# Slot blocks, residual adds and projections in a two-layer graph kernel

## Chip, core and metric

The kernel runs on one core of a Trainium2 chip. The metric is the device time of one execution in microseconds, the median of repeated runs; a profile is one more execution, recorded by the hardware profiler.

The core's engines run side by side and meet through semaphores: PE (TensorE, matrix products into PSUM), DVE (VectorE), ACT (ScalarE), POOL (GpSimd) and SP (which issues the DMAs). Each takes its instructions strictly in the order in which the program lists them, so an instruction that waits holds up all behind it on its engine.

## What is computed

128 graphs of 128 nodes with 64 features each. `adj` is a weighted adjacency; about one entry in sixteen is not zero. Layer 0 sums, over the neighbours k of node j, a hidden vector of 192 ReLUs, and projects the sum; layer 1 is a matrix product with `adj` and a small network. Both are residual with a layer norm.

```python
mask = (adj > 0.0)
xj_proj = x @ W1a
diff = x[:, :, None, :] - x[:, None, :, :]
h = relu(xj_proj[:, :, None, :] + diff @ W1b + b1)      # 128 x 128 x 192 a graph
hm = einsum('bjkh,bjk->bjh', h, mask)
x = layernorm(x + hm @ W2 + deg[..., None] * b2)
...
agg = einsum('bmn,bnd->bmd', adj, x)
h = elu(agg @ V1 + c1); h = elu(h @ V2 + c2)
out = layernorm(x + h @ V3 + c3)
```

The argument of the ReLU is A[j] + C[k], with A = x (W1a + W1b) + b1 and C = -x W1b. So layer 0 needs, for each node and each of its neighbours, relu(A[j] + C[k]).

## The kernel before, in words

**Pairs and slots.** Two graphs make a pair; there are 64 pairs, and the work is laid out by pair. `prepare` finds each node's degree, ranks the nodes by it and builds a permutation (`permb`, `permT`); `sort_x` and `sort_mask` sort features and mask, so that node position 0 has the most neighbours. A node at sorted position p gets a fixed number of slots, one for each neighbour it may have, from the table

```python
BANKS = (((72, 128, 9),), ((30, 72, 12),), ((0, 8, 22), (8, 30, 15)))
```

An entry (p0, p1, s) is a block: positions p0 to p1 with s slots each, s x (p1 - p0) columns. The blocks of one inner tuple share a PSUM bank[...]. In all E = 1514 columns.

**One-hot columns.** `sort_mask` computes with a prefix matmul the running number of each neighbour (`vp`), and compares it on DVE with each slot's number (`slotc`): `oh` (L572) has a one where neighbour k of position p falls into slot s. One compare per block, for both graphs at once.

**Units.** The hidden dimension is cut in three columns c: 0 and 1 are the first 128 channels of either graph, 2 holds the last 64 of both. A unit is (pair, c, bank): nine a pair. ACT seeds the bank `e` with A[j], repeated over the slots (L714, one instruction per block); PE adds C[k] by gathering with the one-hot columns, three bf16 parts of C in turn (L725 for c = 0 and 1, three matmuls; L729 for c = 2, six half-width ones); DVE reduces |A + C| over the slots (L739, one instruction per block). Since relu(z) = (z + |z|)/2 the linear part is added later, and an empty slot leaves |A|. What empty slots contribute is taken off by `corr`: `short` (L520 to L528) builds with matmuls 2 x (slots - degree), PSUM gets it by a constant matmul of `small` with `srow2` (L523) and by matmuls of -2 with the sorted mask (L525, L527); DVE multiplies by max(A, 0) (L532), POOL subtracts A x slots (L518, L538). Four banks (`edges`, NE = 4) go round, so four units are under way.

**Projection of A.** `project_a` (L498) computes A for the three columns by three matmuls of all 128 rows with zero-padded weights `wap` and `wah` (L504) into one bank, and ACT adds b1 in two instructions (L509, L511).

**Finish.** `finish` (L636): POOL forms hm (L642) from the sums and corr once the pair's nine units are reduced, PE projects with W2, ACT copies, and `unsort` (L661) puts the rows back in the order of the input, adding x by a matmul with the identity (L662). `norm` (L594) copies the result out on ACT (L597), takes the statistics on DVE from PSUM (L603, L605), POOL raises to -1/2 (L610), DVE and ACT apply (L613, L619). Then come the product with `adj` (`aggregate`), two ELU layers (`hidden1`, `hidden2`) and `last` (L692), which adds x1 again by an identity matmul (L694), and the second `norm`.

**The order.** No scheduler of the compiler decides it. `Flow` is a planner in the kernel: each step names its engine, an assumed cost in us, what it comes after and how many of the four general PSUM banks (`m0` to `m3`) it takes. It emits the step that can start first by its own clock, among near ones the one due first. ROUND (13.0) sets the pace at which pairs are due, AHEAD = 3 how many pairs earlier preparation begins. "POOL PORT" and "DVE PORT" steps are kept apart on the planner's clock. The emitted order is fixed; on the chip each engine follows it. `load` issues a pair's two DMAs, `finish` the two stores.

**The dense part.** Where a node had more neighbours than slots, `dense` would compute its pair again without slots; it starts with a test over all pairs (L792 to L800).

Of the kernel before, what the change touches and what calls it, by code (L numbers as in the profile page):

```python
# [39 lines left out]
EPS = 1e-5  # L40


BANKS = (((72, 128, 9),), ((30, 72, 12),), ((0, 8, 22), (8, 30, 15)))


@with_exitstack
def gnn_kernel(ctx: ExitStack, tc: tile.TileContext, x, adj, w1, b1, w2, b2,
# [74 lines left out]
    nc.vector.memset(onesf, 1.0)  # L122
    onesb = const([P, 2 * P], BF16, "onesb")
    nc.vector.memset(onesb, 1.0)
    small = const([P, P], BF16, "small")
    nc.vector.memset(small, 1.0 / P)
# [5 lines left out]
    mtwoh = const([P, 2, P], BF16, "mtwoh")  # L132
    nc.vector.memset(mtwoh, 0.0)
    for s in range(2):
        nc.vector.memset(mtwoh[:, s, s * HB:(s + 1) * HB], -2.0)
    mone = const([P, 1], F32, "mone")
    nc.vector.memset(mone, -1.0)

# [45 lines left out]
    srow2 = const([P, 3, P], BF16, "srow2")  # L184
    nc.vector.tensor_scalar(srow2, srow, 2.0, None, op0=OP.mult)

    wa = temp([P, H], F32, "wa")
# [162 lines left out]
def sparse(tc, env):  # L350
# [18 lines left out]
    EV = {}  # L369


    ROUND = 13.0
    AHEAD = 3
    PACE = ROUND / (3 * NB)
    STEP = 1.3
# [34 lines left out]
    def flat(t):  # L410
        return t.rearrange("p s n -> p (s n)")

    def prepare(p):

        a = ADJ[p]
        d = S[p] = {}
        mk = d["mk"] = prep.tile([P, 2, N], BF16, name="mk")
        ev, = yield ("POOL PORT", pool(2 * N) + 0.2, [event("load", p)], 0,
                     lambda: nc.gpsimd.tensor_scalar(mk, a, 0.0, None, op0=OP.is_gt))  # L419
        deg = prep.tile([P, 2], F32, name="deg")  # L420
        ev, = yield ("DVE", dve(2 * N), [ev], 0,
                     lambda: nc.vector.tensor_reduce(deg, mk, AX.X, OP.add))
# [24 lines left out]

        def permute():
            for s in range(2):
                nc.vector.tensor_scalar(permb[:, s, :], g.iotb, pos[:, s:s + 1], None,  # L450
                                        op0=OP.is_equal)
        ev, = yield ("DVE PORT", 0.36, [ev], 0, permute)
        flow.start(due(p, 7), STEP, sort_x(p, ev))
        flow.start(due(p, 7), STEP, sort_mask(p, ev))

# [42 lines left out]
    def project_a(p, xT, ev):  # L498

        d = S[p]  # L500

        def project(aps):
            for c, w in enumerate((g.wap[:, 0, :], g.wap[:, 1, :], g.wah)):
                nc.tensor.matmul(aps[:, c * N:(c + 1) * N], w, xT[:, 1, :], start=True, stop=True)  # L504
        ev, aps = yield ("PE", 0.66, [ev], 1, project)
        aj = d["aj"] = prep.tile([P, 3, N], F32, name="aj", bufs=6)

        def bias():
            nc.scalar.activation(flat(aj[:, 0:2, :]), aps[:, :2 * N], AF.Identity,  # L509
                                 bias=g.b1c[:, 0:1])  # L510
            nc.scalar.activation(aj[:, 2, :], aps[:, 2 * N:3 * N], AF.Identity,  # L511
                                 bias=g.b1c[:, 1:2])
        ev, = yield ("ACT", act(2 * N, 1) + act(N, 1), [ev], 0, bias)
        flow.give(aps, ev)
        happened(ev, "aj", p)
        have = ev
        sa = prep.tile([P, 3, N], F32, name="sa")
        evs, = yield ("POOL PORT", 1.0, [have], 0, lambda: nc.gpsimd.tensor_mul(sa, aj, g.srow))  # L518

        def short(eb):  # L520

            mtp = d["mtp"]
            nc.tensor.matmul(eb[:, :3 * N], g.small, g.srow2.rearrange("p c n -> p (c n)"),  # L523
                             start=True, stop=False)
            nc.tensor.matmul(eb[:, :2 * N], g.mtwo, flat(mtp), start=False, stop=False)  # L525
            for s in range(2):
                nc.tensor.matmul(eb[:, 2 * N:3 * N], g.mtwoh[:, s, :], mtp[:, s, :],  # L527
                                 start=False, stop=(s == 1))  # L528
        ev, eb = yield ("PE", 0.38, [have, event("mtp", p)], 1, short)
        ea = prep.tile([P, 3, N], F32, name="ea")  # L530
        ev, = yield ("DVE", dve(3 * N), [ev], 0,
                     lambda: nc.vector.scalar_tensor_tensor(  # L532
                         ea, aj, 0.0, eb[:, :3 * N].rearrange("p (c n) -> p c n", c=3),
                         op0=OP.max, op1=OP.mult))
        flow.give(eb, ev)

        corr = d["corr"] = prep.tile([P, 3, N], F32, name="corr", bufs=7)
        ev, = yield ("POOL PORT", 1.05, [ev, evs], 0, lambda: nc.gpsimd.tensor_sub(corr, ea, sa))  # L538
        happened(ev, "corr", p)

    def sort_mask(p, ev):
# [49 lines left out]
        flow.give(t, ev)  # L591
        happened(ev, "adjT", p)

    def norm(yps, ev, name):  # L594

        y = work.tile([P, 2, O], F32, name="y", bufs=6)
        evy, = yield ("ACT", act(2 * O), [ev], 0, lambda: nc.scalar.copy(flat(y), yps[:, :2 * O]))  # L597
        st = work.tile([P, 2, 3], F32, name="st", bufs=12)
        ve = work.tile([P, 2], F32, name="ve", bufs=12)

        def stats():

            nc.vector.bn_stats(st.rearrange("p s t -> p (s t)"),  # L603
                               yps[:, :2 * F].rearrange("p (s f) -> p f s", s=2))
            nc.vector.tensor_scalar(ve, st[:, :, 2], 1.0 / F, EPS, op0=OP.mult, op1=OP.add)  # L605
        ev, = yield ("DVE", 0.38, [ev, evy], 0, stats)
        flow.give(yps, ev)
        rs = work.tile([P, 2], F32, name="rs", bufs=12)
        ev, = yield ("POOL PORT", 0.72, [ev], 0,
                     lambda: nc.gpsimd.tensor_tensor(rs, ve, g.mhalf, op=OP.pow))  # L610
# [25 lines left out]
    def finish(p):  # L636
# [22 lines left out]
        nc.sync.dma_start(g.degs[:, 2 * p:2 * p + 2], ys[:, 2 * O:])  # L659

        def unsort(t):  # L661
            nc.tensor.matmul(t[:, :2 * O], ident, flat(xx), start=True, stop=False)  # L662
            for s in range(2):
                nc.tensor.matmul(t[:, s * O:(s + 1) * O], d["permT"][:, s, :],  # L664
                                 ys[:, s * O:(s + 1) * O], start=False, stop=(s == 1))
# [25 lines left out]

        def last(t):  # L692
            nc.tensor.matmul(t[:, :2 * O], onesb[:, :P], flat(g.c3p), start=True, stop=False)
            nc.tensor.matmul(t[:, :2 * O], ident, flat(x1), start=False, stop=False)  # L694
            for s in range(2):
                nc.tensor.matmul(t[:, s * O:(s + 1) * O], h2[:, s * N:(s + 1) * N], g.v3s,
                                 start=False, stop=(s == 1))
        ev, t = yield ("PE", 0.83, [ev], 1, last)
# [278 lines left out]
```

## Time and profile before

| | |
|---|---|
| median of 3 runs | 928.74 us (928.43 to 929.03) |
| the profiled execution | 928.32 us |
| its span, first to last instruction | 925.7 us |
| first gather starts, last one ends | 42.2 us, 902.4 us |
| PE busy | 867.1 us (94%), 6739 instructions |
| DVE busy | 813.8 us (88%), 2278 instructions |
| ACT busy | 717.3 us (77%), 2050 instructions |
| POOL busy | 506.6 us (55%), 654 instructions |
| DMA | 18.84 MB, 20 GB/s, q1 8.1% of 16 engines |

The span is a fill (loads, set-up, preparation of the first pairs), 64 rounds of one pair each with all stages of different pairs beside each other, and a drain. Busy is the union of an engine's instructions; PE's ends are modelled, so its starts are the safer reading. In groups by line, the columns behind the bar are busy us, mean ns of one, and idle time of the engine before them with what ended it. DVE's and ACT's instructions overlap the next by some 80 ns where nothing holds it.

### The profile page before, as it was taken

The page shows a single profiled execution, that of the slowest core. Times are in us where ns is not written, and L with a number is a line of the kernel's source. Part 1 is how long each engine was busy: PE and PEld are TensorE (multiplying, and loading weights), DVE is VectorE, ACT ScalarE, POOL GpSimd, SP SyncE. Part 2 cuts the span into 40 slices and gives each one's busy share as a digit, 9 for nine tenths or more (in the row PEclk, how much of TensorE's full clock was granted, in tenths as well). Part 3 has the DMA queues.
Part 4 walks back from the last instruction along what each step waited for, and adds up shares of the span by engine and source line. Part 5 has one row for each costly group of instructions (what it writes and reads, how often), then busy time and mean ns, then how long its engine had stood idle before and what let it go on. Part 6 is the DMA issues. An engine that isn't in the chain of part 4 may idle for free. (4 is left out here: it accounts for less than half of the span.)

```text
span 925.7 us, 19643 instructions
## 1 busy us (share of the span) xinstructions
PE 867.1 (94%) x6739; PEld 556.4 (60%) x6740; DVE 813.8 (88%) x2278; ACT 717.3 (77%) x2050; POOL 506.6 (55%) x654
## 2 busy tenths in 40 slices
PE   2689999999999999999999999999999999999994
PEld 1456666665665665666665666666666666666663
DVE  7699889989989989989989989999999999999972
ACT  0577887788788788788788788888878887888772
POOL 1565555665556565556565556565556555555521
PEclk9999999999999999999999999999999999999996
DMA  1100100100110110110100010110011001000000
GB/s 29 43 10 21 25 15 21 24 21 16 24 24 13 24 24 14 24 25 12 25 23 15 22 24 12 25 24 16 21 25 24 16 21 25 16 23 22 7 8 12
DMA packets 63580, 18.84 MB, mean 20 GB/s; under 512 B 46257, under 2 KB 63474, under 8 KB 63474
## 3 DMA queue, kind: packets, MB, share of 16 engines
q1 hardware_dynamic: 63474, 17.52, 8.1%
q8 instruction: 55, 0.90, 0.4%
q14 instruction: 51, 0.42, 0.1%
HBM read 13.24 MB, written 4.19 MB: 19 GB/s over the span
## 5 line engine op out<-in xcount | busy, mean ns | idle before, releaser
L739 DVE TENSOR_REDUCE sums<-e 128x56 f32<-128x504 f32 (+3 forms) x768 | 395.0, 542 | 33.6 <-PE e L725 16.9
L714 ACT COPY e<-aj 128x504 f32<-128x504 f32 (+2 forms) x768 | 366.1, 486 | 74.3 <-DVE sums L739 67.4
L725 PE MATMUL e<-oh,cp 128*128 128x504 bf16 (+1 forms) x1152 | 281.7, 375 | 1.8 <-ACT e L714 1.7
L610 POOL TENSOR_TENSOR rs<-ve,mhalf 128x2 f32<-128x2 f32 x128 | 90.6, 708 | 228.2 <-DVE ve L605 223.9
L725 PEld LDWEIGHTS <-cp 128*128 128x128 bf16 x1152 | 106.1, 97 | 89.5 <-DVE sums L739 1.1
L729 PE MATMUL e<-oh,cp 128*64 128x504 bf16 (+1 forms) x1152 | 157.5, 382 | 1.1 <-ACT e L714 1.1
L572 DVE TENSOR_TENSOR oh<-vp,slotc 128x1008 bf16<-128x1008 bf16 (+2 forms) x256 | 153.9, 601 | 3.2 <-ACT vp L564 3.0
L642 POOL TENSOR_TENSOR hm<-sums,corr 128x384 f32<-128x384 f32 x64 | 73.6, 1151 | 45.8 <-DVE sums L739 42.3
L629 ACT ACTIVATE e<-m,mone 128x256 f32<-128x256 f32 x128 | 62.6, 489 | 32.4 <-PE m L688 30.9
L493 POOL CAST cp<-r 128x512 bf16<-128x512 f32 x64 | 48.9, 765 | 70.5 <-DVE r L490 70.4
L729 PEld LDWEIGHTS <-cp 128*64 128x64 bf16 x1152 | 53.9, 109 | 42.9 <-issue 18.2
L495 POOL TENSOR_TENSOR cp<-r,cp 128x512 bf16<-128x512 f32 x64 | 74.5, 1164 | 5.0
L518 POOL TENSOR_TENSOR sa<-aj,srow 128x384 f32<-128x384 f32 x64 | 64.4, 1007 | 21.2 <-ACT aj L511 21.1
L538 POOL TENSOR_TENSOR corr<-ea,sa 128x384 f32<-128x384 f32 x64 | 67.2, 1050 | 3.6 <-DVE ea L532 2.6
L419 POOL TENSOR_SCALAR mk<-adj 128x256 bf16<-128x256 f32 x64 | 54.8, 856 | 21.3 <-DMA xx<-in_x_dram 20.9
L632 DVE SCALAR_TENSOR_TENSOR h<-e,m 128x256 f32<-128x256 f32 x128 | 52.5, 410 | 10.1 <-ACT e L629 9.3
L490 DVE TENSOR_TENSOR r<-m,cp 128x256 f32<-128x256 f32 x128 | 53.1, 416 | 6.5 <-ACT cp L486 6.1
L597 ACT COPY y<-m 128x128 f32<-128x128 f32 x128 | 33.4, 261 | 28.7 <-PE m L664 22.0
L619 ACT ACTIVATE o<-y,nb,rs 128x64 f32<-128x64 f32 x128 | 51.2, 467 | 3.0 <-DVE nb L613 3.0
L486 ACT CAST cp<-m 128x256 bf16<-128x256 f32 x128 | 49.5, 388 | 3.2 <-PE m L479 3.2
L619 ACT ACTIVATE x<-y,nb,rs 128x64 f32<-128x64 f32 x128 | 49.3, 433 | 3.3 <-DVE nb L613 1.6
L651 PE MATMUL m<-w2h,hm 128*128 128x64 f32 x256 | 48.1, 289 | 0.0
(189 smaller groups left out, 1731.5 us busy)
## 6 DMA issues: line engine op xcount, KB each, us to landing
adj<-in_adj_dram SPq DMA_DIRECT2D x64, 128.0 KB, 2.3
xx<-in_x_dram SPq DMA_DIRECT2D x64, 64.0 KB, 2.2
out_dram<-o SPq DMA_DIRECT2D x64, 64.0 KB, 1.7
degs<-ys SPq DMA_DIRECT2D x64, 1.0 KB, 1.7
w1a<-in_L_gnn_W_dram SPq DMA_DIRECT2D x2, 48.0 KB, 2.2
w1b<-in_L_gnn_W_dram SPq DMA_DIRECT2D x2, 48.0 KB, 2.1
v1d<-in_L_gnn_W_dram SPq DMA_DIRECT2D x2, 32.0 KB, 2.1
v2s<-in_L_gnn_W_dram SPq DMA_DIRECT2D x1, 64.0 KB, 2.0
```

The lines of the kernel that those rows point to most:

```text
L495: lambda: nc.gpsimd.tensor_sub(cp[:, 2], r1, cp[:, 1]))
L518: evs, = yield ("POOL PORT", 1.0, [have], 0, lambda: nc.gpsimd.tensor_mul(sa, aj, g.srow))
L538: ev, = yield ("POOL PORT", 1.05, [ev, evs], 0, lambda: nc.gpsimd.tensor_sub(corr, ea, sa))
L572: lambda: nc.vector.tensor_tensor(oh[:, :, c].rearrange("p b (s w) -> p b s w", w=w), vp[:, :, p0:p1].rearrange("p b (o w) -> p b o w", o= ...
L610: lambda: nc.gpsimd.tensor_tensor(rs, ve, g.mhalf, op=OP.pow))
L619: nc.scalar.activation(o[:, s, :], y[:, s, :], AF.Identity, bias=nb[:, s:s + 1], scale=rs[:, s:s + 1])
L629: lambda: nc.scalar.activation(e, z, AF.Exp, bias=g.mone))
L642: lambda: nc.gpsimd.tensor_sub(hm, d["sums"], d["corr"]))
L714: nc.scalar.copy(e[:, off:off + sl * w].rearrange("p (s w) -> p s w", w=w), d["aj"][:, c:c + 1, p0:p1].to_broadcast([P, sl, w]))
L725: nc.tensor.matmul(e[:, :n], cp[:, k, c, 0:P], oh[:, c, base:base + n], start=False, stop=(k == 2), skip_group_check=True)
L729: nc.tensor.matmul(e[s * HB:(s + 1) * HB, :n], cp[:, k, s, P:H], oh[:, s, base:base + n], start=False, stop=(k == 2), skip_group_check=True)
L739: nc.vector.tensor_reduce(d["sums"][:, c, p0:p1], e[:, off:off + sl * w].rearrange("p (s w) -> p w s", w=w), AX.X, OP.add, apply_absolute_ ...
```

## The change

- **Six blocks.** Still three banks, now each with two blocks; E = 1355 columns. Seeds, compares and reductions are one instruction per block, so eighteen, six and eighteen a pair.
- **Residuals on POOL.** `unsort` and `last` lose the identity matmul. `norm` gets `rest`: ACT copies PSUM into y and gives the bank back, POOL adds `rest`, DVE takes the statistics from y.
- **A by row tiles.** For c = 0 and 1 two matmuls of 64 rows each, on the two halves of the array's rows, into two banks; `wah` as before; ACT adds b1 in three instructions.
- **Empty-slot factor.** POOL computes `free` = sorted mask - slots/128 in bf16; `short` is one matmul of -2 with it and two half-width ones. `small`, `srow2`, `mtwoh` go.
- ROUND becomes 11.8, and assumed costs in the planner change with the steps.

```diff
-BANKS = (((72, 128, 9),), ((30, 72, 12),), ((0, 8, 22), (8, 30, 15)))
+BANKS = (((34, 65, 11), (0, 3, 22)), ((65, 99, 9), (3, 15, 16)), ((15, 34, 13), (99, 128, 7)))
...
+    sfrac = const([P, 2, P], BF16, "sfrac")
+    nc.vector.tensor_scalar(sfrac, srow[:, 0:2, :], 1.0 / P, None, op0=OP.mult)
...
-    ROUND = 13.0
+    ROUND = 11.8
...
-        def project(aps):
-            for c, w in enumerate((g.wap[:, 0, :], g.wap[:, 1, :], g.wah)):
-                nc.tensor.matmul(aps[:, c * N:(c + 1) * N], w, xT[:, 1, :], start=True, stop=True)
-        ev, aps = yield ("PE", 0.66, [ev], 1, project)
+        def project(*aps):
+            for s in range(2):
+                k = slice(s * F, (s + 1) * F)
+                nc.tensor.matmul(aps[s][:, 0:N], g.wa[k, 0:P], xT[k, 1, :], start=True, stop=True)
+            nc.tensor.matmul(aps[0][:, N:2 * N], g.wah, xT[:, 1, :], start=True, stop=True)
+        ev, *aps = yield ("PE", 0.5, [ev], 2, project)
...
-            mtp = d["mtp"]
-            nc.tensor.matmul(eb[:, :3 * N], g.small, g.srow2.rearrange("p c n -> p (c n)"),
-                             start=True, stop=False)
-            nc.tensor.matmul(eb[:, :2 * N], g.mtwo, flat(mtp), start=False, stop=False)
-            for s in range(2):
-                nc.tensor.matmul(eb[:, 2 * N:3 * N], g.mtwoh[:, s, :], mtp[:, s, :],
-                                 start=False, stop=(s == 1))
-        ev, eb = yield ("PE", 0.38, [have, event("mtp", p)], 1, short)
+            free = d["free"]
+            nc.tensor.matmul(eb[:, :2 * N], g.mtwo, flat(free), start=True, stop=True)
+            for s in range(2):
+                nc.tensor.matmul(eb[s * HB:(s + 1) * HB, 2 * N:3 * N], g.mtwo[:, :HB],
+                                 free[:, s, :], start=True, stop=True)
+        ev, eb = yield ("PE", 0.2, [have, event("free", p)], 1, short)
...
+        free = d["free"] = prep.tile([P, 2, N], BF16, name="free")
+        evf, = yield ("POOL PORT", 0.7, [evm], 0,
+                      lambda: nc.gpsimd.tensor_sub(free, mtp, g.sfrac))
+        happened(evf, "free", p)
...
-        evy, = yield ("ACT", act(2 * O), [ev], 0, lambda: nc.scalar.copy(flat(y), yps[:, :2 * O]))
+        ev, = yield ("ACT", act(2 * O), [ev], 0, lambda: nc.scalar.copy(flat(y), yps[:, :2 * O]))
+        flow.give(yps, ev)
+        ev, = yield ("POOL PORT", 0.45, [ev], 0, lambda: nc.gpsimd.tensor_add(y, y, rest))
...
             nc.vector.bn_stats(st.rearrange("p s t -> p (s t)"),
-                               yps[:, :2 * F].rearrange("p (s f) -> p f s", s=2))
+                               y.rearrange("p s f -> p f s"))
...
         def unsort(t):
-            nc.tensor.matmul(t[:, :2 * O], ident, flat(xx), start=True, stop=False)
             for s in range(2):
                 nc.tensor.matmul(t[:, s * O:(s + 1) * O], d["permT"][:, s, :],
-                                 ys[:, s * O:(s + 1) * O], start=False, stop=(s == 1))
-        ev, t = yield ("PE", 0.6, [ev, event("permT", p)], 1, unsort)
-        x1, ev = yield from norm(t, ev, "x1")
+                                 ys[:, s * O:(s + 1) * O], start=True, stop=True)
+        ev, t = yield ("PE", 0.42, [ev, event("permT", p)], 1, unsort)
+        x1, ev = yield from norm(t, ev, "x1", xx)
...
             nc.tensor.matmul(t[:, :2 * O], onesb[:, :P], flat(g.c3p), start=True, stop=False)
-            nc.tensor.matmul(t[:, :2 * O], ident, flat(x1), start=False, stop=False)
...
-        o, ev = yield from norm(t, ev, "o")
+        o, ev = yield from norm(t, ev, "o", x1)
```

More of the change, by code (lines that the diff above doesn't have):

```diff
@@ L124, in gnn_kernel @@
     nc.vector.memset(onesb, 1.0)
-    small = const([P, P], BF16, "small")
-    nc.vector.memset(small, 1.0 / P)
     mhalf = const([P, 2], F32, "mhalf")
@@ L131, in gnn_kernel @@
     nc.vector.memset(mtwo, -2.0)
-    mtwoh = const([P, 2, P], BF16, "mtwoh")
-    nc.vector.memset(mtwoh, 0.0)
-    for s in range(2):
-        nc.vector.memset(mtwoh[:, s, s * HB:(s + 1) * HB], -2.0)
     mone = const([P, 1], F32, "mone")
@@ L183, in gnn_kernel @@
         nc.vector.memset(srow[:, :, p0:p1], float(s))
-    srow2 = const([P, 3, P], BF16, "srow2")
-    nc.vector.tensor_scalar(srow2, srow, 2.0, None, op0=OP.mult)
-    wa = temp([P, H], F32, "wa")
+    sfrac = const([P, 2, P], BF16, "sfrac")
+    nc.vector.tensor_scalar(sfrac, srow[:, 0:2, :], 1.0 / P, None, op0=OP.mult)
+    wa = const([P, H], F32, "wa")
     nc.vector.tensor_add(wa, w1a, w1b)
@@ L451, in permute @@
                                         op0=OP.is_equal)
-        ev, = yield ("DVE PORT", 0.36, [ev], 0, permute)
+        ev, = yield ("DVE PORT", 0.45, [ev], 0, permute)
         flow.start(due(p, 7), STEP, sort_x(p, ev))
@@ L500, in project_a @@
         d = S[p]
-        def project(aps):
-            for c, w in enumerate((g.wap[:, 0, :], g.wap[:, 1, :], g.wah)):
-                nc.tensor.matmul(aps[:, c * N:(c + 1) * N], w, xT[:, 1, :], start=True, stop=True)
-        ev, aps = yield ("PE", 0.66, [ev], 1, project)
+        def project(*aps):
[4 more added lines that the diff above has]
+        ev, *aps = yield ("PE", 0.5, [ev], 2, project)
         aj = d["aj"] = prep.tile([P, 3, N], F32, name="aj", bufs=6)
         def bias():
[L509 to L514, printed above, removed]
+            for c in range(3):
+                nc.scalar.activation(aj[:, c, :], aps[c % 2][:, (c // 2) * N:(c // 2 + 1) * N],
+                                     AF.Identity, bias=g.b1c[:, c // 2:c // 2 + 1])
+        ev, = yield ("ACT", 3 * act(N, 1), [ev], 0, bias)
+        for t in aps:
+            flow.give(t, ev)
         happened(ev, "aj", p)
@@ L592, in turn, with norm @@
         happened(ev, "adjT", p)
-    def norm(yps, ev, name):
+    def norm(yps, ev, name, rest):
         y = work.tile([P, 2, O], F32, name="y", bufs=6)
-        evy, = yield ("ACT", act(2 * O), [ev], 0, lambda: nc.scalar.copy(flat(y), yps[:, :2 * O]))
+        ev, = yield ("ACT", act(2 * O), [ev], 0, lambda: nc.scalar.copy(flat(y), yps[:, :2 * O]))
+        flow.give(yps, ev)
+        ev, = yield ("POOL PORT", 0.45, [ev], 0, lambda: nc.gpsimd.tensor_add(y, y, rest))
         st = work.tile([P, 2, 3], F32, name="st", bufs=12)
@@ L603, in stats @@
             nc.vector.bn_stats(st.rearrange("p s t -> p (s t)"),
-                               yps[:, :2 * F].rearrange("p (s f) -> p f s", s=2))
+                               y.rearrange("p s f -> p f s"))
             nc.vector.tensor_scalar(ve, st[:, :, 2], 1.0 / F, EPS, op0=OP.mult, op1=OP.add)
-        ev, = yield ("DVE", 0.38, [ev, evy], 0, stats)
-        flow.give(yps, ev)
+        ev, = yield ("DVE", 0.4, [ev], 0, stats)
         rs = work.tile([P, 2], F32, name="rs", bufs=12)
@@ L697, in last @@
                                  start=False, stop=(s == 1))
-        ev, t = yield ("PE", 0.83, [ev], 1, last)
-        o, ev = yield from norm(t, ev, "o")
+        ev, t = yield ("PE", 0.54, [ev], 1, last)
+        o, ev = yield from norm(t, ev, "o", x1)
         nc.sync.dma_start(g.out[2 * p:2 * p + 2].rearrange("b j f -> j b f"), o)
```

## The prediction

> **What bounds the kernel now.** I read the busy times first, then the windows of the steady part (600 to 800 us), the waits of PE and DVE in it, the timeline of PE over some microseconds and last the groups by shape.
>
> ```profile
> 600.00:800.00 200.00, 197.74 (x1574) 128.23 (x1569) 182.77 (x510) 165.07 (x480) 116.00 (x150) 1.00 0.09 21
> ```
>
> The columns are PE, weight loads, DVE, ACT, POOL, then granted clock and DMA. PE is busy 98.9%, DVE 91.4%, ACT 82.5%, POOL 58%. Since the ends of matmuls are modelled, 98.9% alone proves nothing; the starts do.
>
> ```profile
> 314.11 0.80 PE L725 MATMUL e<-oh,cp 128*128 128x504 bf16 x3
> 314.75 0.41 PE L646 MATMUL m<-w2d,hm 128*128 128x128 f32 x2
> 315.00 0.25 PE L650 MATMUL m<-cp,mtp 128*128 128x64 bf16 x3
> ```
>
> Three gathers of 504 columns start 0.64 us before the next work does: 213 ns each, and the next instruction starts at once. PE works without a break. In the same 200 us it waited 1.2 us in all, while DVE's longest waits are
>
> ```profile
> DVE deg L422 <- POOL mk L419: 7.2, 15, 0.5
> DVE sums L739 <- PE e L729: 4.2, 16, 0.3
> DVE sums L739 <- PE e L725: 2.5, 15, 0.2
> ```
>
> So PE bounds, DVE follows 7% behind. One pair of graphs is one round; its end shows on POOL:
>
> ```profile
> 603.79 1.37 POOL L642 TENSOR_TENSOR hm<-sums,corr 128x384 f32<-128x384 f32 x1 [0.68 <-DVE sums L739]
> ...
> 617.17 1.37 POOL L642 TENSOR_TENSOR hm<-sums,corr 128x384 f32<-128x384 f32 x1 [0.68 <-DVE sums L739]
> ```
>
> 13.38 us per round here. L642 runs from 55.3 to 903.4 us, 63 rounds of 13.46 on the average (about 13.86 between 313 and 550 us). So the span is 55.3 + 63 x 13.46 + 22.3 = 925.7, and the profiled run 928.32, 2.6 more; the median shown, 928.74, is 0.4 above it. A change counts as one from 0.2% (1.9 us). Work per round, DVE and POOL less their 20 and 8 us of set-up: PE 867/64 = 13.5, DVE 794/64 = 12.4, ACT 717/64 = 11.2, POOL 499/64 = 7.8 us.
>
> [...] reductions of 176 and 504 columns last 332 and about 673 ns, which is 148 + n/0.96, and the next op starts about 80 ns before the end, so one more op costs some 68 ns. [...] In before all block widths are even; 1008 elements in 672 ns show the rate, odd widths no run shows. [...] L613, two SBUF inputs, lasts 141 ns at least and 361 at most, L605 168 to 832. [...] four passes of L477 in row tiles take 0.63 us, two full passes of the same width at L688 0.43.
>
> **The change part by part**, per round.
>
> *Six blocks.* E falls from 9x56+12x42+22x8+15x22 = 1514 columns to 1355, 159 less. PE: the gathers of L725 need 6 x 159 / 2.4 = 0.40 us less (504 columns in 213 ns), the half-width ones of column c = 2, two at a time, half of that, 0.20. DVE reductions: 3 x 159/0.96 = 497 ns less, but 6 more ops x 68 = 408 more: -0.09. Slot compares: 2 x 159/1.92 = 166 less, 2 more ops 136: -0.03, if the odd widths (31, 3, 19, 29) keep the double rate. ACT seeds: 3 x 159/1.2 = 398 less; six more at a fixed part of 171 ns (591 - 420) less some 80 of overlap, 546 more: +0.15. Sorted degrees of the reference's inputs stay within the new slots at every position (7 from 99 on, 9, 11, 13, 16, 22 at the top), so the dense part still runs for no pair.
>
> *Residuals on POOL.* PE loses the identity matmuls (start, length; PE's timeline):
>
> ```profile
> 302.40 0.38 PE L662 MATMUL m<-xx,ident 128*128 128x128 f32 x2
> 302.69 0.66 PE L664 MATMUL m<-ys,permT 128*128 128x64 f32 x4
> ...
> 308.78 0.44 PE L694 MATMUL m<-x,ident 128*128 128x128 f32 x2
> 309.06 0.56 PE L696 MATMUL m<-v3s,h 128*128 128x64 f32 x4
> ```
>
> start to start 0.29 (0.22 in another round) and 0.28: I take 0.53. POOL gains two adds of 128 columns. From 128x384 in 1007 ns and 128x2 in 203 a column costs 2.1 ns, so 0.47 us each, 0.94 together. The statistics now follow copy and add, 0.5 us plus two hand-offs later; the next rounds cover that, as nothing carries from pair to pair but buffers. But DVE runs in order: behind a statistic that waits for POOL stand reductions, for which ACT's seeds and PE wait. In the changed order POOL's adds stand behind hm, which waits for the last sums, or behind the 1.16 us of L495. In before POOL's answers (L610) cost DVE 8.1 us in the run; now two answers per norm. I take another 0.1. The statistics read SBUF instead of PSUM, in steps of 64 elements: not shown; from -0.1 to +0.2, I take +0.05.
>
> *Empty-slot factor.* L523, L525 and L527 start at 303.93, 304.10 and 304.21, the next at 304.32: 0.39 us. L525's 0.11 stays, the two halves become two half-width ones at once, 0.06: -0.20. POOL gains `free`, 256 columns: 203 + 254 x 2.1 = 0.74, plus a hand-off ahead of `short`; the lead of three pairs (AHEAD) with which pairs are prepared covers it.
>
> *A by row tiles.* Now 313.44 to 314.11: 0.67. The first two, half the rows, beside each other: 0.22 instead of 0.45, so 0.45 in all, -0.22. Bounds 0 (no overlap) to -0.22. ACT: three biases of 0.36 instead of 0.47 + 0.36, less overlap: +0.17. One bank more of the four for a moment, which y's earlier return pays for.
>
> *Sums.* PE: -(0.60 + 0.53 + 0.20 + 0.22) = -1.55, so 13.5 becomes 11.95. ACT 11.2 + 0.3 = 11.5. POOL 7.8 + 0.94 + 0.74 = 9.5. DVE: -0.12 + 0.05. [...] The groups (busy us, mean ns, then idle before):
>
> ```profile
> L572 DVE TENSOR_TENSOR oh<-vp,slotc 128x1008 bf16<-128x1008 bf16 x128 | 98.7, 771 | 3.1 <-ACT vp L564 3.0
> ...
> L605 DVE TENSOR_SCALAR ve<-st 128x2 f32<-128x2 f32 x128 | 34.3, 268 | 4.4
> ...
> L613 DVE SCALAR_TENSOR_TENSOR nb<-st,rs 128x2 f32<-128x2 f32 x128 | 30.6, 239 | 9.7 <-POOL rs L610 8.1
> ...
> L450 DVE TENSOR_SCALAR permb<-iotb,pos 128x128 bf16<-128x128 bf16 x128 | 29.5, 272 | 0.0
> ```
>
> Means against shortest: 0.10 x 2 for L605 (268 to 168), 0.10 x 2 for L613 (239 to 141), 0.1 x 2 for the wide compares (771; 672 is the median over all of L572) and 0.03 x 2 for L450 (272 to 238): 0.66 us a round. POOL's share goes from 58% to 9.5/12.8 = 74%, so it grows by 0.18, bounds 0 and 0.4. DVE: 12.4 - 0.12 + 0.05 + 0.18 = 12.5. So DVE takes PE's place. PE reached 98.9% as the bound; with the waits named, I give DVE 97.5%: 12.8 per round.
>
> Time: 55.3 + 63 x 12.8 + 22.3 + 2.6 = **887 us**, 41 below the profiled run. Head and tail stay: the first round is set by the chain of one pair, which gains two POOL steps of 0.5 us and loses some matmuls.
>
> **The rivals.**
>
> *A: DVE pays nothing.* POOL's share doesn't hurt, the order fits: DVE 12.2 (its share in 600 to 800: 0.914 x 13.38) and PE 11.95 set 12.3 a round: 855 us. For it: PE kept 98.9%. Against: a sixth more DVE instructions and a busier POOL. Chance 0.15.
>
> *B: waits take the gain.* DVE and ACT stand in line behind POOL's adds, a static order made for rounds of 11.8 meets 12.5; DVE is busy 94%: 13.3 a round, 918 us. For it: in before the first half ran at 13.86 and the second at 13.37, with the same instructions, so order costs half a microsecond. Against: DVE's waits for POOL are small now. Chance 0.18.
>
> *C, the other side: odd widths break the compare's double rate.* Four of the six blocks have odd widths, most rows start on odd elements. If L572 falls to one element a cycle, its 2710 columns cost 2.82 instead of 1.41 us: DVE 12.5 + 1.41 = 13.9, and with 97.5% 14.3 a round, 981 us; if only the four odd blocks (2 x 857 columns, of which half is lost, 0.89 us) fall, 13.75, 947 us. It decides from 0.66 us a round on, 13.46 against 12.8. For it: the trace shows no odd width. [...] Chance 0.12 (the milder form the likelier).
>
> That the change doesn't do what it says I hold for unlikely: the changed instruction order shows six compares, eighteen reductions and no identity matmul per pair.
>
> **How the numbers follow.** 0.55 for the forecast (872 to 903 alone), 0.15 A, 0.18 B, 0.12 C. The unknown DVE terms (statistics -0.1 to +0.2[...]) set DVE between 12.2 and 12.9 us a round before waits. The range takes in A and B and leaves C out: 854 to 922. Faster than 0.2%: 0.55 + 0.15 + nearly all of B = 0.86; within: 0.02; slower 0.12.
>
> **What would show it.** PE's busy share falls below 95% and its waits become waits for ACT's seeds and DVE; DVE's rises to 96% or more; 31- and 34-wide reductions last 148 + n/0.96; the compare of 2 x 306 about 467 ns and of 2 x 341 (odd) about 503 if the rate holds, over 850 if not; POOL near 74%; rounds of 12.8 between hm's. A round at 13.4 or more, or L613 and L605 far above 0.3 us on the average, would make it wrong.

## The result and the profile after

| | before | after |
|---|---|---|
| median of four runs | 928.59 us | 932.23 us |
| ratio after to before, 95% | | 1.0041 (1.0023 to 1.0058) |
| profiled run / its span | 928.32 / 925.7 | 932.87 / 931.1 |
| first and last hm on POOL (L642) | 55.3 / 903.4 | 58.0 / 907.4 |
| round, whole run (last less first, by 63) | 13.46 us | 13.48 us |

The forecast was 887 us, in a range of 854 to 922. The change made the kernel slightly slower. First the windows of the changed kernel; the columns are length, then busy time of PE, weight loads, DVE, ACT and POOL.

```profile
600.00:800.00 200.00, 188.07 (x1466) 115.28 (x1465) 187.26 (x615) 176.55 (x574) 132.93 (x192) 1.00 0.09 20
100.00:800.00 700.00, 659.70 (x5154) 406.42 (x5153) 658.66 (x2163) 617.33 (x2012) 462.50 (x672) 1.00 0.09 21
```

PE fell from 98.9% to 94.0%, as it should; but DVE did not rise to 97.5%, it stands at 93.6%. No engine is busy all the time now. The groups of the changed kernel on DVE and POOL, in the columns used before:

```profile
L571 DVE TENSOR_TENSOR oh<-vp,slotc 128x682 bf16<-128x682 bf16 (+5 forms) x384 | 170.6, 444 | 4.9 <-ACT vp L563 1.5
L606 DVE TENSOR_SCALAR ve<-st 128x2 f32<-128x2 f32 x128 | 51.8, 404 | 4.4
L444 DVE TENSOR_SCALAR permb<-iotb,pos 128x128 bf16<-128x128 bf16 x128 | 47.6, 413 | 0.0
L613 DVE SCALAR_TENSOR_TENSOR nb<-st,rs 128x2 f32<-128x2 f32 x128 | 38.8, 303 | 2.9 <-POOL rs L610 2.9
...
L598 POOL TENSOR_TENSOR y<-y,x 128x128 f32<-128x128 f32 x64 | 32.9, 514 | 31.2 <-ACT y L596 31.2
L554 POOL TENSOR_TENSOR free<-mtp,sfrac 128x256 bf16<-128x256 bf16 x64 | 44.9, 701 | 37.1 <-ACT mtp L549 37.1
```

POOL's new steps cost about what was written down: the additions 0.51 and 0.46 us for 0.47 each, `free` 0.70 for 0.74. But ve, two elements a partition, rose from 268 to 404 ns, permb from 272 to 413, nb from 239 to 303. One such case in the timeline (start, length):

```profile
705.39 1.16 POOL L489 TENSOR_TENSOR cp<-r,cp 128x512 bf16<-128x512 f32 x1
705.45 0.28 DVE L604 BATCH_NORM_STATS2 st<-y 128x6 f32<-128x128 f32 x1
705.76 0.82 DVE L606 TENSOR_SCALAR ve<-st 128x2 f32<-128x2 f32 x1
...
706.50 0.48 DVE L571 TENSOR_TENSOR oh<-vp,slotc 128x612 bf16<-128x612 bf16 x1
```

POOL's subtraction ends at 706.55, and ve, which needs 0.17 alone, at 706.58: it ended when POOL did. The other ve show the same. Of the 103 ve between 100 and 800 us, 27 began while POOL was idle, and these lasted 169 to 172 ns. 60 lasted over 228 ns, and every one of them ended 23 to 28 ns after a POOL instruction that was under way when it began (L489 26 times, L532 25, L642 8, L514 once). The other 16 met POOL's short degb or keyc (L421, L422) and lasted 169 to 195 ns. In the kernel before, 68 of 103 began beside an idle POOL, and the 35 long ones all ended with L495.

So in both traces ve cost what the POOL instruction beside it left: 168 to 172 ns beside an idle POOL, else up to 951. For nb it isn't always so: in the kernel before, nb (141 ns at least) met POOL's mk, of 856 ns, 51 times in this stretch, took 346 to 353 ns and ended 441 to 447 ns before it.

Where did POOL's wait go? The largest waits of POOL between 100 and 800 us, before and then after (total us, times, longest):

```profile
POOL rs L610 <- DVE ve L605: 172.8, 68, 3.5
POOL cp L493 <- DVE r L490: 60.9, 35, 3.0
```

```profile
POOL hm L642 <- DVE sums L737: 58.9, 44, 2.8
POOL sa L514 <- ACT aj L506: 55.0, 52, 2.4
...
POOL rs L610 <- DVE ve L606: 19.2, 27, 1.3
```

Of the 294 us in which POOL was idle in that stretch of before (42% of 700), it stood 172.8 at its root, waiting for ve, and its 68 waits there are the 68 ve that ran beside a POOL at rest. In the new order POOL hardly waits there; often it is still at an earlier, long instruction. Part of the burden changed sides: POOL's own hm fell from 1151 to 1020 ns, its cast (L493, now L487) from 765 to 636, degb from 413 to 225.

### The profile page after: what moved, and what is told of

Read it like the earlier page. It is cut to its first block, busy times and chain, and to the rows that moved or that the text cites. A ratio compares the mean times of both kernels' runs of the same rounds, so it can differ in the third digit from the quotient of the medians.

```text
span 931.1 us, 20393 instructions
## 1 busy us (share of the span) xinstructions
PE 838.7 (90%) x6419; PEld 512.7 (55%) x6420; DVE 842.9 (91%) x2792; ACT 769.7 (83%) x2498; POOL 578.8 (62%) x848
## 5 line engine op out<-in xcount | busy, mean ns | idle before, releaser
L712 ACT COPY e<-aj 128x341 f32<-128x341 f32 (+5 forms) x1152 | 406.6, 359 | 55.9 <-DVE sums L737 34.7
L737 DVE TENSOR_REDUCE sums<-e 128x31 f32<-128x341 f32 (+5 forms) x1152 | 381.7, 380 | 25.1 <-PE e L723 22.5
L723 PE MATMUL e<-oh,cp 128*128 128x407 bf16 (+2 forms) x1152 | 278.5, 357 | 0.3 <-ACT e L712 0.3
L571 DVE TENSOR_TENSOR oh<-vp,slotc 128x682 bf16<-128x682 bf16 (+5 forms) x384 | 170.6, 444 | 4.9 <-ACT vp L563 1.5
L727 PE MATMUL e<-oh,cp 128*64 128x407 bf16 (+2 forms) x1152 | 142.7, 359 | 13.6 <-ACT e L712 13.2
L514 POOL TENSOR_TENSOR sa<-aj,srow 128x384 f32<-128x384 f32 x64 | 64.1, 1002 | 76.8 <-ACT aj L506 76.8
L642 POOL TENSOR_TENSOR hm<-sums,corr 128x384 f32<-128x384 f32 x64 | 65.3, 1020 | 72.7 <-DVE sums L737 70.4
L532 POOL TENSOR_TENSOR corr<-ea,sa 128x384 f32<-128x384 f32 x64 | 68.3, 1067 | 16.4 <-DVE ea L526 15.9
L489 POOL TENSOR_TENSOR cp<-r,cp 128x512 bf16<-128x512 f32 x64 | 74.3, 1161 | 3.0
L506 ACT ACTIVATE aj<-m,b1c 128x128 f32<-128x128 f32 x192 | 56.4, 365 | 17.2 <-PE m L500 15.6
L554 POOL TENSOR_TENSOR free<-mtp,sfrac 128x256 bf16<-128x256 bf16 x64 | 44.9, 701 | 37.1 <-ACT mtp L549 37.1
L487 POOL CAST cp<-r 128x512 bf16<-128x512 f32 x64 | 40.7, 636 | 31.4 <-DVE r L484 31.4
L454 ACT CAST permf<-permb 128x256 f32<-128x256 bf16 x64 | 25.8, 403 | 40.0 <-DVE permb L444 39.7
L606 DVE TENSOR_SCALAR ve<-st 128x2 f32<-128x2 f32 x128 | 51.8, 404 | 4.4
```

The source lines that it names most:

```text
L489: lambda: nc.gpsimd.tensor_sub(cp[:, 2], r1, cp[:, 1]))
L506: nc.scalar.activation(aj[:, c, :], aps[c % 2][:, (c // 2) * N:(c // 2 + 1) * N], AF.Identity, bias=g.b1c[:, c // 2:c // 2 + 1])
L571: lambda: nc.vector.tensor_tensor(oh[:, :, c].rearrange("p b (s w) -> p b s w", w=w), vp[:, :, p0:p1].rearrange("p b (o w) -> p b o w", o= ...
L642: lambda: nc.gpsimd.tensor_sub(hm, d["sums"], d["corr"]))
L712: nc.scalar.copy(e[:, off:off + sl * w].rearrange("p (s w) -> p s w", w=w), d["aj"][:, c:c + 1, p0:p1].to_broadcast([P, sl, w]))
L723: nc.tensor.matmul(e[:, :n], cp[:, k, c, 0:P], oh[:, c, base:base + n], start=False, stop=(k == 2), skip_group_check=True)
```

## The experiments

Two measures are used throughout. The first is the *excess* of DVE: the length of each DVE instruction above the shortest tenth of its shape, counted where over 60 ns, between 100 and 800 us, per round. R is the round in the same stretch (13.63 before, 13.58 after, some 0.1 to 0.2 above the round of the whole run). Both are worked out from the trace. Where even the shortest tenth of a shape was held up, as with ve in e3, the excess comes out too low. The excess was 0.66 us before and is 1.33 after: +0.67 where the prediction had +0.18, at most +0.4.

The second is the *chain*: from the last instruction before 800 us back to 100 us, at each step to what released the instruction, or, where nothing did, to the one before it on its engine. In the kernel before it lies on PE for 69% of the time, on DVE for 15% and on ACT for 13%; in the changed kernel on PE for 49%, DVE 29%, ACT 12% and POOL 5%.

The theories that the expectations name: T1, the amount of POOL's work makes DVE's instructions longer; T2, the planned order and its waits; T3, the smaller block instructions cost more than they save; T4, the borders between full-array and part-array matmuls eat PE's savings in A and in `short` (0.75 us against 0.67 for A, 0.38 against 0.39 for `short`); T5, the chain alternates between PE and DVE, and what DVE's small operations lose where they meet long ones of POOL lies on it; T6, PE's queue alone sets the round. "Held" means that the planned order is that of the changed kernel.

**e1, POOL's additions not issued** (order held; the residuals are left out).

```diff
-        ev, = yield ("POOL PORT", 0.45, [ev], 0, lambda: nc.gpsimd.tensor_add(y, y, rest))
+        ev, = yield ("POOL PORT", 0.45, [ev], 0, lambda: None)
```

> The changed kernel with its order of instructions held, but POOL's two residual adds a pair not issued (the residuals are left out of the result). T1[...]: 0.97 us less POOL work a round takes DVE's excess on L444, L571, L606 and L613 from 1.39 us a round to about 1.0 and DVE's busy share stays the bound: rounds of 13.1, about 900 us. T2, the fixed order makes engines wait for each other whatever POOL does: the order is the same, so 924 to 932. T3, the cost of more and smaller block instructions on DVE and ACT: no change, 930 to 932.

926.76 us, 0.9983 (0.9977 to 0.9990). Only 5 us less than the changed kernel. POOL's share fell from 66% to 60%, the excess stayed at 1.32, and ve even rose:

```profile
L606 DVE TENSOR_SCALAR ve<-st 128x2 f32<-128x2 f32 x128 | 60.0, 468 | 4.4
```

T1, which wanted about 900 us and an excess near 1.0, falls: it isn't the amount of work. POOL's wait at the root is 22.8 us, as small as with the additions: the order set it.

**e2, e1 plus the identity matmuls again** (order held).

```diff
+            nc.tensor.matmul(t[:, :2 * O], ident, flat(xx), start=True, stop=False)
...
+            nc.tensor.matmul(t[:, :2 * O], ident, flat(x1), start=False, stop=False)
```

> As e1, but with the residuals added by identity matmuls on PE again (0.53 us of PE work a round), order of all else held. T1: as e1, since PE has that room: 898 to 906. T2: PE's 0.53 us falls into a chain that passes through PE for half its length: 932 to 945. T3: 930 to 935.

955.07 us, 1.0288 (1.0270 to 1.0305): 28 us above e1, 0.45 a round, and above every range that was written down (T2's, the nearest, ended at 945). By the starts, in the median of all rounds, the two steps with the residuals take 0.44 us longer than in e1. So PE's work still counts in full, at a PE that is busy 94.7%. "DVE takes PE's place" was wrong.

**e3, the blocks of before in the changed kernel; e4, the new blocks alone in the kernel before** (both planned anew; `BANKS` alone is exchanged).

> The changed kernel with the four blocks of before. T1: DVE's work rises by 0.1 us a round and PE's by 0.6, POOL stays: 935 to 950. T2: a new order, anything within 20 us of 932. T3, small block instructions cost more than their columns save: faster than 925.

> The kernel before with the six blocks alone. T1: PE loses 0.6 us a round, POOL does what it did, DVE's excess stays near 0.67: rounds of 12.8 to 13.0, 890 to 900 us. T2: about 928, as the order is as ill fitted as before. T3: 928 to 940, the gain of PE is eaten by DVE and ACT.

e3: 965.86 us, 1.0408 (1.0391 to 1.0426). e4: 918.18 us, 0.9896 (0.9879 to 0.9912). Both lie outside all that was expected: e3 above 952, e4 between 900 and 928. T3 falls with e4: the blocks alone gain 10 us. The 34 us of e3 are not the blocks' alone. Its new order is the clearest case of the wait for POOL: no ve began beside an idle POOL, all 98 in the stretch ended with L532 or L642, with POOL busy 65% as in the changed kernel:

```profile
L606 DVE TENSOR_SCALAR ve<-st 128x2 f32<-128x2 f32 x128 | 90.6, 708 | 4.4
```

Measured from the shortest ve of the other runs (168 ns), e3's excess is 2.1 us a round.

In e4 DVE's work fell from 12.42 to 12.11 a round, ve was down to 186 ns, and POOL waited 228.9 us at its root. That this gain of 10 us is only 0.31 a round (R 13.32), where PE should save 0.60 and its gathers take 0.57 less by their starts, is explained in part: the chain lies on DVE for 35% of the time there, on PE for 51%. PE shows 98.6% all the same, but with ends that are modelled.

**e5, A by full rows; e6, `short` with its constant matmul** (order held).

```diff
-                nc.tensor.matmul(aps[s][:, 0:N], g.wa[k, 0:P], xT[k, 1, :], start=True, stop=True)
+                nc.tensor.matmul(aps[s][:, 0:N], g.wap[:, s, :], xT[:, 1, :], start=True, stop=True)
```

```diff
+            nc.tensor.matmul(eb[:, :3 * N], g.small, g.srow2.rearrange("p c n -> p (c n)"), start=True, stop=False)
...
-                nc.tensor.matmul(eb[s * HB:(s + 1) * HB, 2 * N:3 * N], g.mtwo[:, :HB],
+                nc.tensor.matmul(eb[:, 2 * N:3 * N], g.mtwoh[:, s, :], free[:, s, :],
...
-        free = d["free"] = prep.tile([P, 2, N], BF16, name="free")
+        d["free"] = mtp
...
-                      lambda: nc.gpsimd.tensor_sub(free, mtp, g.sfrac))
+                      lambda: None)
```

> The changed kernel with A's first two matmuls over all 128 rows with padded weights again, in the same two banks and the same order. T4, row tiles save PE nothing here, as the trace of the changed kernel suggests (L499 and L500 take 0.76 us a round, L504 took 0.69): equal or faster, 925 to 932. If the tiles save 0.2 us a round, as the prediction had it, PE's loss shows: 938 to 946.

> The changed kernel with the empty-slot factor by the constant matmul of before, POOL's subtraction not issued, order held. T4, the switch to half-width tiles and back eats what the shorter matmuls save (L519 and L521 take 0.39 us a round, as L523 to L527 did): PE is the same and POOL loses 0.7 us: 922 to 931. As predicted (PE 0.2 us a round more): 936 to 945. T1, POOL's work counts: 915 or below.

e5: 936.04 us, 1.0083 (1.0066 to 1.0100), 4 us above the changed kernel and between the two ranges: the row tiles are worth 0.06 us a round, not 0.22. e6: 930.96 us, 1.0027 (1.0017 to 1.0037), 1.3 below it, as T4 had it: the new `short` saves nothing. PE's timeline of the changed kernel shows why:

```profile
701.44 0.49 PE L499 MATMUL m<-xT,wa 64*128 64x128 f32 x4
701.86 0.49 PE L500 MATMUL m<-xT,wah 128*128 128x128 f32 x2
702.19 0.68 PE L723 MATMUL e<-oh,cp 128*128 128x407 bf16 x3
...
703.73 0.27 PE L519 MATMUL m<-free,mtwo 128*128 128x256 bf16 x1
703.93 0.25 PE L521 MATMUL m<-free,mtwo 128*64 128x128 bf16 x2
704.11 0.28 PE L686 MATMUL m<-onesb,c2p 128*128 128x256 bf16 x1
```

Start to start, the four row-tile passes take 0.42, and at full rows took 0.45; the two after them take 0.33 instead of 0.22. In all 0.75 against 0.67 before. `short` takes 0.20 + 0.18 = 0.38, against 0.39 before (the medians of all rounds agree with these starts): the constant matmul is gone, but L519 lasts 0.20 until the half-width tiles start, where 256 bf16 columns took 0.11. So at each of the two borders between full-array and part-array matmuls some 0.1 us more was measured (0.33 for 0.22, 0.20 for 0.11); what causes it, no run separates. T4 holds: of 1.55 us 1.13 was left at most.

**e7, e8: only the round length that the planner aims at is exchanged** (`ROUND` 11.8 to 13.0 in the changed kernel, 13.0 to 11.8 in the one before).

> The changed kernel planned with the pace of before (ROUND 13.0 instead of 11.8), not one instruction more or less. T2, what decides is how the fixed order lets DVE's and PE's steps meet: the time moves by more than 5 us either way, down to 905 if the pace nearer to the chip's fits better. T1 and T3: within 3 us of 932.

> The kernel before planned with ROUND 11.8. T2: another order, the time moves by more than 5 us, up to 950. T1 and T3: within 3 us of 928.

e7: 936.77 us, 1.0083 (1.0066 to 1.0101). e8: 938.80 us, 1.0114 (1.0097 to 1.0131). **e11: the planner keeps the statistics and nb, too, apart from POOL's steps** ("DVE" becomes "DVE PORT" at L607 and L612, and nb's assumed cost 0.1 becomes 0.15).

> The changed kernel with two labels in the planner[...]. Only the order changes. T5: DVE's excess falls below 1.0 us a round and the time to 905 to 928, unless the new order makes worse waits elsewhere. T6: 925 to 945, as any other order.

945.20 us, 1.0168 (1.0151 to 1.0185), 13 above the changed kernel, where T5 had hoped for 905 to 928: ve fell to 251 ns, but permb rose to 620. So order alone, at the same instructions, moves the time by 4.5 to 13 us, as much as the parts of this change; so far T2 holds. The excess does not order these runs: 1.11, 0.97 and 1.49. In e8 ve is at 176 ns, and yet it is slower than before. A new order changes more than these waits.

**e12, the residuals on POOL alone, in the kernel before** (planned anew; identity matmuls removed, `norm` with the addition).

> The kernel before with POOL's residual adds alone (four blocks, A and the empty-slot factor as before). PE loses 0.53 us a round, POOL gains 0.97, statistics wait for POOL. T6: PE's queue sets the round, 895 to 905. T5: part of it, and the new order's share of DVE's waits, 905 to 930. T1: slower than 932.

931.93 us, 1.0026 (1.0016 to 1.0037), above the ranges of T5 and T6: this part alone gives nothing for 0.53 us of PE. The excess rose from 0.66 to 1.06, POOL's wait at the root fell from 172.8 to 54.0 us. The parts do not add up: about -10 (blocks) and +3 (residuals) alone, -4 (A) and +1 (`short`) by undoing them in the changed kernel, make -10 us, against +4 for the whole.

**e9, ve on POOL instead of DVE; e10, two long POOL instructions cut** (order held). e9 gives POOL more to do and takes DVE's most hindered operation away; e10 changes no work, only how long one instruction of POOL lasts.

```diff
-            nc.vector.tensor_scalar(ve, st[:, :, 2], 1.0 / F, EPS, op0=OP.mult, op1=OP.add)
+            nc.gpsimd.tensor_scalar(ve, st[:, :, 2], 1.0 / F, EPS, op0=OP.mult, op1=OP.add)
```

```diff
-                     lambda: nc.gpsimd.tensor_sub(cp[:, 2], r1, cp[:, 1]))
+                     lambda: [nc.gpsimd.tensor_sub(cp[:, 2, s], r1[:, s], cp[:, 1, s])
+                              for s in range(2)])
...
-        ev, = yield ("POOL PORT", 1.05, [ev, evs], 0, lambda: nc.gpsimd.tensor_sub(corr, ea, sa))
+        ev, = yield ("POOL PORT", 1.05, [ev, evs], 0, lambda: [nc.gpsimd.tensor_sub(corr[:, c], ea[:, c], sa[:, c])
+                              for c in range(3)])
```

> The changed kernel with the small DVE operation that forms variance + eps (L606, twice a pair, mean 400 ns for 169 of work) done by POOL in the step of its root; order of all else held. T5, the chain that sets the round alternates between PE and DVE[...]: DVE loses 0.6 us a round, 0.3 to 0.6 of it shows, 897 to 915. T6, PE's queue alone sets the round: 927 to 934. T1, POOL's amount of work holds DVE up: POOL works 0.4 us more, 932 or more.

> The changed kernel with two long POOL instructions cut up in place: L489 (1.16 us) in two, L532 (1.07 us) in three, so POOL works some 0.45 us more a round[...]; order held. T5: DVE waits to the end of the POOL instruction that it meets, so its excess falls from 1.35 us a round to 0.9 or less and the time to 905 to 922. T1: POOL's amount of work decides, 935 to 950. T6: 930 to 936.

e9: 910.89 us, 0.9801 (0.9785 to 0.9818). e10: 919.17 us, 0.9886 (0.9869 to 0.9902). Both times lie in T5's ranges. The excess of e9 stayed at 1.33, though: what ve no longer waits, the compares and nb wait in its place (the compares 0.49 a round instead of 0.19), and the gain is that DVE has less to do. In e10 the excess fell to 1.19 only, where 0.9 was expected. POOL works longer there (71% against 66%), and ve is back at 273 ns:

```profile
L608 DVE TENSOR_SCALAR ve<-st 128x2 f32<-128x2 f32 x128 | 35.0, 273 | 4.4
```

**e13, e10 and also hm (L642) in three and free (L554) in two pieces; e14, e9 and e10 together** (order held).

> e10 with L642 (hm) in three and L554 (free) in two as well: POOL works 0.6 us a round more than in e10[...]; order held. T5: DVE's excess falls from e10's 1.19 us a round to about 0.9, 908 to 917. T1, POOL's amount of work: 922 or more.

> e9 and e10 together. T5: the gains add in part, 895 to 906. T6, PE's queue takes over at once: 908 to 912.

e13: 906.50 us, 0.9768 (0.9752 to 0.9785). e14: 911.43 us, 0.9826 (0.9809 to 0.9842), no better than e9 alone: T5 missed here, T6's range was hit, and why the two gains don't add is not shown. (Not all of POOL's instructions are short in e13: sa, L515, keeps its 1.0 us.) e13's groups and window:

```profile
L609 DVE TENSOR_SCALAR ve<-st 128x2 f32<-128x2 f32 x128 | 29.8, 233 | 4.4
...
L645 POOL TENSOR_TENSOR hm<-sums,corr 128x128 f32<-128x128 f32 x192 | 92.0, 501 | 15.0 <-DVE sums L741 15.0
```

```profile
100.00:800.00 700.00, 674.63 (x5305) 414.08 (x5304) 660.19 (x2229) 634.54 (x2069) 531.16 (x1009) 1.00 0.09 21
```

POOL has more to do than in any run up to here (75.9%), DVE the same operations in the same order as in the changed kernel, and the time falls by 26 us. The excess fell to 1.02. This speaks most plainly against T1 and for T5, whose range it beat a little. It isn't all in the excess, though: 0.31 us of it stands against 0.39 of R; whether hm in pieces also hands on its first part sooner, no run separates.

**e15, e9 and nb on POOL too; e16, e15 with the cuts of e10; e17, e15 with those of e13** (order held).

```diff
+            nc.gpsimd.tensor_scalar(nm, st[:, :, 1], -1.0, None, op0=OP.mult)
+            nc.gpsimd.tensor_tensor(nb, nm, rs, op=OP.mult)
...
-                     lambda: nc.vector.scalar_tensor_tensor(nb, st[:, :, 1], -1.0, rs,
-                                                            op0=OP.mult, op1=OP.mult))
+                     lambda: None)
```

> e9 with nb (L613) formed by POOL too, in two small operations behind the root; DVE keeps neither of norm's small operations; order held. POOL works 0.8 us a round more than in e9. T5: DVE loses another 0.3 us base and 0.4 of excess a round; with PE at some 12.5 us a round 890 to 903. T1, or POOL's longer stay in norm's chain: 911 or more.

> e15 with e10's cuts. T5: 882 to 898, PE's share at 97% or more. If POOL (some 80% busy) becomes the queue that others wait for: 905 or more.

> e15 with the cuts of e13 (L489 in two, L532 and L642 in three, L554 in two), order held. e16 showed 896 with PE 98.2% busy. T5: PE's queue sets the round by now, so little is left: 888 to 897. If POOL, then some 87% busy, holds others up: 897 to 910.

e15: 900.65 us, 0.9699 (0.9683 to 0.9715). e16: **896.00 us, 0.9649 (0.9633 to 0.9665)**, the best. e17: 897.17 us, 0.9664 (0.9646 to 0.9681). e16's window, and its largest wait on DVE there:

```profile
100.00:800.00 700.00, 687.52 (x5385) 420.99 (x5384) 627.94 (x2046) 642.63 (x2098) 586.28 (x1186) 1.00 0.09 22
```

```profile
DVE sums L745 <- PE e L731: 28.3, 62, 0.9
```

The excess is 0.57, DVE's work 11.68 a round at 89.7%, PE is at 98.2% and DVE waits for PE's gathers again, at R 13.02: PE is the fullest engine once more, though the chain lies on it for 53% of the time only (DVE 19%, ACT 15%, POOL 9%). More cuts (e17, POOL 86%) bring nothing further.

**e18, cuts like e13's in the kernel before** (L495 in two, L538 and L642 in three pieces).

> The kernel before with L495 in two, L538 and L642 in three pieces. T5: PE's queue is full (98.9%), DVE's excess (0.66 us a round) lies beside it, so cuts bring little: 922 to 930. If the cuts help in another way, as in e13: 905 to 915.

933.28 us, 1.0048 (1.0030 to 1.0066): 5 us slower, and above both ranges. POOL's share rose from 58.0 to 62.5%, the excess stayed (0.71 after 0.66): ve fell only from 268 to 246 ns, permb rose from 272 to 297. POOL still rested 156.1 us at its root, so there was little to win, and PE stood at 98.0%. The cut is no gain in itself.

## Why the prediction was wrong

*What bounds the kernel before, and PE's relief as the first effect*: right. PE fell from 98.9% to 94.0% and DVE's share rose.

*PE's saving of 1.55 us*: 0.42 of it was never there. Both small terms, A by row tiles (-0.22) and `short` (-0.20), gave about nothing (e5, e6, and the starts above). That two matmuls of half the rows run beside each other in half the time was the author's estimate; four such passes took 0.42 us where full rows took 0.45. The bound 0 for A had been written down; for `short` none had. The two large terms came out smaller, too. By the medians of the starts the residuals' 0.53 is 0.44 (e1 and e2, 28 us), and the blocks' 0.60 is 0.57 in e4, where R fell by 0.31 only, and 0.40 in the order of the changed kernel. So some 0.8 to 0.9 us of the 1.55 were there.

*ACT, +0.3*: too small. ACT's work rose from 11.17 to 11.99 us a round in the stretch. The sum took some 80 ns of overlap off each added seed. But where two seeds go to one bank, the second starts some 32 ns after the end of the first, in all 192 cases of before and all 576 after. So six more take some 0.2 us each (171 + 32 ns), less the 0.40 of the columns.

*DVE, -0.12 for the blocks, +0.05 for the statistics*: the sizes of single instructions were right, and the blocks were better than said (-0.31 in e4, of which 0.08 is excess). The statistics last 285 ns from SBUF (L604, mean) and lasted 288 from PSUM (L603, before).

*DVE, +0.18, its excess scaled with POOL's share*: **this step failed first**. The scale was the author's estimate; the excess rose by 0.67. It doesn't scale with POOL's share: at 60% it was 1.32 (e1), at 76% 1.02 (e13), at 84% 0.57 (e16, with fewer DVE operations there). It follows from where in a fixed order DVE's small operations meet a long POOL instruction: ve lost nothing where POOL was idle, and ended 23 to 28 ns after POOL's instruction where it met a long one. The row that could have told it was in the trace of before: POOL waited 172.8 us for ve at its root. That rest was the cover under which 68 of 103 ve ran, and ve cost 268 ns in the mean. In each kernel that was planned without the additions (before, e4, e8, e18) it is 156 to 229 us, in each that was planned with them (after, e7, e11, e12) 19 to 67, in e3 none at all, and e1 shows that leaving the additions out of a finished plan doesn't bring it back. It covers ve alone: in e8 ve cost 176 ns, but the compares were held up for 0.66 us a round.

*"DVE takes PE's place, busy 97.5%"*: **this step failed second**. DVE's work came to 12.78 a round, 0.28 more than 12.5; its idle time to 0.80, where 2.5% of 12.8 is 0.32. Together 0.76 us, nearly the difference between 12.8 forecast and R 13.58. Idle time stayed because no single engine set the round: PE and DVE are both at 94%, more of PE's work costs time in full (e2), and less of DVE's gives it in full (e9: DVE's work falls by 0.34 a round, R by 0.33). The chain crosses between them (PE 49%, DVE 29%, ACT 12%), which makes it longer than the work of either alone. Not every order shows it so: in e14 DVE's work is 0.1 below e9's and R is not. A sum per engine, with the larger one as the bound, cannot show that.

*The rivals.* B was nearest: DVE busy 94%, waits in line behind POOL. But it priced the wait at 13.3 with DVE's work at 12.5; 12.78 / 0.941 is 13.58. A fell. C did not come about, as the groups by shape of the changed kernel show:

```profile
L571 DVE TENSOR_TENSOR oh<-vp,slotc 128x682 bf16<-128x682 bf16 x64 | 34.3, 535 | 1.5 <-ACT vp L563 1.5
L737 DVE TENSOR_REDUCE sums<-e 128x31 f32<-128x341 f32 x192 | 96.8, 504 | 11.1 <-PE e L723 10.1
```

The compare in rows of 31 lasts 535 ns in the mean (508 in its shortest tenth; 503 was said), the reduction 504 (503 said). The other side was reached on another path: the small loss is what DVE's instructions lose beside POOL's, together with an order that suits the new work less.

*Head and tail*: the first hm came 2.7 us later (58.0), the tail took 23.7 instead of 22.3. "Head and tail stay" was off by 4 of the 45 us.

What stays open: how the 0.8 us of idle time splits between PE's queue, ACT and the order; why the planner's order for the changed kernel leaves POOL so little rest at the root; and why the cuts add nothing to e9. No run changed ACT's work, so what its 0.8 us cost is not known. A theory that only PE's queue sets the round (T6) does not fit e9 to e16, in which PE's instructions stay as they are and the time falls by up to 36 us.

## What to carry to other kernels

Before work is put on an engine beside which instructions of a nearly full one were seen to last longer (ve here, to the end of POOL's in 60 of 103 cases), look at the waits of the receiving engine: a long wait for a tiny operation of the other (172.8 us for ve here) is rest that the other lives on. Here it was lost in every order that was planned with the new steps, and leaving their work out did not bring it back. Price such waits by the longest instruction that stands nearby, not by a share of busy time; where they do lie on the chain, cutting that instruction, or moving the tiny operation across, gets the gain back (932 to 896 us here), and where PE was full and POOL at rest it cost time (e18). When two engines come within some per cent of each other in a fixed order (PE 94.2% and DVE 94.1% of the stretch here), expect both to be idle a little, and give the round a value above the work of either.

## What the runs showed of the hardware

- A DVE operation on two elements a partition (ve) lasted from 169 to 951 ns in the changed kernel. In the stretch it lasted 169 to 172 beside an idle POOL (27 cases); the 60 long ones ended 23 to 28 ns after the POOL instruction that they met.
- Not every meeting lasts to the end: before, nb (two SBUF inputs, 141 ns at least) met POOL's mk (L419, one input, 856 ns) 51 times in the stretch, took 346 to 353 ns and ended 441 to 447 ns before it.
- Two ACT seeds of one PSUM bank stood 31 to 33 ns apart in all 192 cases of before and all 576 of the changed kernel; where one bank's second seed met the next bank's first without a wait, the two overlapped by some 65 ns (medians 64 to 66).
- More POOL work, in shorter instructions, made the kernel faster: 66% to 76% busy, 932.2 to 906.5 us (e13), at 501 ns a piece where the whole of hm had taken 1020.
- fp32 matmuls on 64 rows, on the two halves of the array, took 0.42 us for four passes of 128 columns, nearly as much as full rows take (0.45); the full-array matmul after them and the one before half-width tiles took about 0.1 us longer than in the kernel before (0.33 for 0.22, and 0.20 for 0.11).
- Rows of odd length, about half of them on odd starts, kept the rate of the 2-byte compare: 682 elements in rows of 31 took 508 ns in the shortest tenth, 132 in rows of 3 took 235, so about 0.50 ns an element; from 352 to 1008 elements in even rows (before) it was 0.53, in the reductions from 66 to 341 columns 1.05.
- In both traces the instructions of the rounds start in the order in which the program lists them: on ACT all 2048 of before and 2496 of the changed kernel, on POOL all 640 and 832, and on DVE and PE all of the lines that leave one record an instruction (1920 and 4032, 2432 and 3968).
